# Conditioned two-stage block on one core: inner weight sums stored behind the second slot tile, and other places for the second group's transposes and outer sums

## The chip, the cores and the metric

The kernel runs on one core of a Trainium2 chip. A core has five engines with an instruction stream each: TensorE (PE; its weight loads, PEld, overlap matmuls), VectorE (DVE), ScalarE (ACT), GpSimd (POOL) and SyncE (SP), which here only issues transfers. ACT and POOL issue transfers too. Within an engine, instructions are taken in order; engines wait for each other, and for transfers, on semaphores. The metric is the device time of one execution in microseconds.

## What is computed

The input is 32 sequences of 128 tokens with 512 features, a condition vector for each sequence, and a mask. All is float32.

```python
m = mask[:, :, None]
shift, scale, gate_msa = jnp.split(silu(t) @ ada_w + ada_b, 3, axis=1)
norm = jnp.where(m, layernorm(x) * (1 + scale[:, None]) + shift[:, None], 0.0)
fwd = gelu(norm @ ssm_w1 + ssm_b1) @ ssm_w2 + ssm_b2
bwd = flip(gelu(flip(norm) @ bwd_w1 + bwd_b1) @ bwd_w2 + bwd_b2)
x = x + gate_msa[:, None] * jnp.where(m, fwd + bwd, 0.0)
shift_mlp, scale_mlp, gate_mlp = jnp.split(silu(t) @ ffada_w + ffada_b, 3, axis=1)
ff_norm = layernorm(x) * (1 + scale_mlp[:, None]) + shift_mlp[:, None]
h = gelu_tanh(ff_norm @ ff_w1 + ff_b1)
return x + gate_mlp[:, None] * (h @ ff_w2 + ff_b2)
```

The first half changes x only where the mask is set, and each token is treated alone. The second half is a feed-forward block (512 to 1024 to 512) over all 4096 tokens. The mask of this input is set at the padded tails of the sequences, a minority of the tokens.

## The kernel before, in words

**First half, on slots.** The masked tokens are numbered and packed into slots, 128 to a tile. Two tiles (0 and 1) are always done, two more (2 and 3) after them; later ones, if the mask asks for any, in a loop at the end. A slot tile is gathered from x, normalised and modulated (`modulated`), transposed (`transposed_slots`), put through the hidden layer (`hidden`: matmuls into a PSUM tile, GELU on ACT) and the projection (`project`, line 202: eight feature blocks of two matmuls each accumulate into one PSUM tile `po`). `finish_slots` and `keep_slots` then form the new token rows on DVE in three steps, bias (line 208), gate (line 210) and x (line 301), and store them in a DRAM tensor `x1_rows` (line 303): tiles 0 and 1 by the ACT queue, 2 and 3 by the SP queue.

**Second half, by pairs of groups.** The 32 sequences form eight groups of four; a pair p holds two groups. For each pair x is loaded (`load_side`, line 332) and the tokens that the first half changed are overwritten by indirect gathers from `x1_rows` on POOL (`take_first_half`, line 666). For pair 0 these can come only from the first 256 slots, so they wait for slot tiles 0 and 1 alone; those of pair 1 need tiles 2 and 3 too. Then come statistics (lines 698 to 704: variance on DVE, the power on POOL) and normalising (710). Group 0 is turned to feature rows by DVE blocks and transfers (`turned`, 737); group 1 of pair 0 by PE: `transposed` (line 726) writes four transposes for one block of features into a PSUM tile and DVE scales and shifts them into `xT[1]` (line 718).

**Fewer products.** Each of the two matrix products of a pair is done by a seven-product scheme on 2 x 2 blocks, and the first of them is done in two levels. The outer level forms sums of the token blocks (`TokenBlocks.one`, line 767: s1 = a21 + a22, s2 = s1 - a11, a21 = a11 - a21, s4 = a12 - s2) and of the weights. Two of the outer level's token blocks live in `s12`: P5 reads s1, P6 reads s2, and P1 and P2 read the plain `xT[0]`. The inner level, within each outer product, has sums of weight sums: `weight_sums(j)` for j = 1 to 4 makes seven blocks each on DVE (line 586) and stores them to DRAM (`t_rows`, lines 587 and 588: 512 KB and 384 KB), from which `load_weights` (line 844) brings them back. The buffers of sum 1 are two x tiles, reused by sum 4; sum 2 lies in the buffers of later fw2 sums, and sum 3 in the buffer `xn`, which group 0's normalised tokens take next.

`FirstProduct` runs seven streams (products of the inner level), each over the seven outer products (`phase`, line 898). The opening, written out by hand, is: product P1 of stream 1 and its seed (line 944), P1 of stream 2, then P2, P5 and P6 of stream 1, and so on. PSUM has three tile pools: `ps_t` (2 buffers, transposes), `ps_h` (3) and `ps_o` (3). A projection, and the accumulator `a` of a stream, come from `ps_o`; a new tile waits for the last reader of the buffer that it takes.

**What sets the order.** From the start of the first half to the end of the straight part everything stands under a manual schedule: each of the five engines runs its instructions in program order. A transfer takes one of eight completion semaphores in turn and waits until the transfer that had this semaphore before has landed, whichever queue issued it.

The opening of the second half, as the change finds it, is this:

```python
    finish_slots(2, h1, gs[0])
    po = project(1, h1, w2, "s3", {1: turn(0), 3: turn(1), 5: turn(2), 7: turn(3)})
    of_x[0] = TokenBlocks(0, xT)
    keep_slots(3, po, gs[1], lambda: of_x[0].one(1))
    for j in (2, 3):
        of_x[0].one(j)
```

`turn(k)` is the transpose of feature block k of group 1; the number in front is the feature block of the projection ahead of which it stands.

Of the kernel before, what the change touches and what calls it, by code (L numbers as in the profile page):

```python
# [22 lines left out]
def kernel(  # L23
# [49 lines left out]
    nc = tc.nc  # L73
# [70 lines left out]
    w2 = ssm.tile([P, HC, D], F32, name="w2")  # L144
# [18 lines left out]
    def group_of_tiles(name):  # L163
        return xnp.tile([P, G, D], F32, tag="xn", name=f"xn_{name}")
# [17 lines left out]
    def hidden(xT, n, w, bcol, func, name, pool, parts=range(HC)):  # L182

        h = []
        for f in parts:
            ph = ps_h.tile([P, 512], F32, tag="h", name=f"ph_{name}_{f}")
            for k in range(KC):
                nc.tensor.matmul(  # L188
                    ph[:, :n], w[:, k, ts(f, P)], xT[:, k, :], start=(k == 0), stop=(k == KC - 1)
                )  # L190
            t = pool.tile([P, n], F32, tag="h", name=f"h_{name}_{f}", bufs=HC + 2)
            nc.scalar.activation(t, ph[:, :n], func, bias=biasT[:, bcol + f : bcol + f + 1])  # L192
            h.append(t)
        return h

    def project(i, h, w, name, between=None):

        po = ps_o.tile([P, 512], F32, tag="o", name=f"po_{name}_{i}")
        for f in range(HC):
            if between and f in between:  # L200
                between[f]()
            nc.tensor.matmul(po, h[f][:, ts(i, P)], w[:, f, :], start=(f == 0), stop=(f == HC - 1))  # L202
        return po

    def gated(po, bias, gate, name, between=lambda: None):

        t = tp.tile([P, D], F32, tag="t", name=f"t_{name}")
        nc.vector.tensor_tensor(t, po, bias, ALU.add)
        between()
        nc.vector.tensor_tensor(t, t, gate, ALU.mult)  # L210
        return t

# [75 lines left out]
    def slot_part(at, j, pool, tag):  # L288
        return of_slots(pick, at, mod1, j, pool, tag, f"part{j}_s{at}")

    def keep_gate(at, gate):
        t = ssm.tile([P, D], F32, tag="gs", name=f"gs_{at}", bufs=2)
        nc.scalar.copy(t, gate)
        return t

    def finish_slots(at, h1, gate, between=None):
        keep_slots(at, project(at % (NC // 2), h1, w2, f"s{at}", between), gate)

    def keep_slots(at, po, gate, between=lambda: None):
        t = gated(po, b2, gate, f"s_{at}", between)  # L300
        nc.vector.tensor_tensor(t, t, xc[at], ALU.add)
        queue = nc.scalar if at < NC // 2 else nc.sync
        queue.dma_start(x1_rows[ts(at, P), :], t)
# [212 lines left out]
    b2 = ssm.tile([P, D], F32, name="b2")  # L516
# [43 lines left out]
    t_rows = dram.tile([4, P, 7, 2 * P], F32, name="t_rows")  # L560
    spare = [x_tile(f"{2 * G}_{n}") for n in range(2)]

    def in_blocks(t):
        return t.rearrange("p g (h f) -> p (g h) f", f=2 * P)

    t_sum = {
        1: [in_blocks(t) for t in spare],
        2: [t_2[:, 0], t_2[:, 2]],
    }
    t_sum[4] = t_sum[1]  # L570

    def sum_block(j, n):
        t = t_sum[j]
        return t[1][:, :3] if n == 2 else t[0][:, 2 * n : 2 * n + 2]

    def weight_sums(j):

        for n in range(3):
            b11, b12, b21, b22 = of_w.quarters(n, (0, 0), (0, 1), (1, 0), (1, 1))
            x, y = {  # L580
                1: lambda: (b12, b11),
                2: lambda: (b22, sum_block(1, n)),
                3: lambda: (b22, b12),
                4: lambda: (b21, sum_block(2, n)),
            }[j]()
            nc.vector.tensor_tensor(sum_block(j, n), x, y, ALU.subtract)
        nc.sync.dma_start(t_rows[j - 1, :, :4], t_sum[j][0])
        nc.sync.dma_start(t_rows[j - 1, :, 4:], t_sum[j][1][:, :3])


    h1 = []
    gs = []
    xn_s = []
    for c in range(2):
# [7 lines left out]
        if c == 1:  # L602
            transposed_slots(xn_s[0], xT_t[:, :, ts(0, P)], "s2")
    weight_sums(1)
    nc.vector.tensor_tensor(b2, b2, b2b, ALU.add)
    b2_row = dram.tile([1, D], F32, name="b2_row")
    nc.sync.dma_start(b2_row, b2[0:1, :])
    weight_sums(2)
    finish_slots(0, h1, gs[0])
    transposed_slots(xn_s[1], xT_t[:, :, ts(1, P)], "s3")  # L610
    t = in_blocks(group_of_tiles("tw_3"))
    t_sum[3] = [t[:, :4], t[:, 4:]]
    weight_sums(3)
    fw2_of = Weights(fw2, HC // 2, D // 2, t_2)
    fw2_of.combine(0, 1)
    nc.vector.tensor_scalar(modb_f[B : 2 * B], modb_f[B : 2 * B], 1.0, None, ALU.add)
    finish_slots(1, h1, gs[1])

    mod2 = const.tile([3 * B, D], F32, name="mod2")
    pm = ps_o.tile([P, 512], F32, tag="o", name="pm_f")  # L620
# [4 lines left out]
    gs = [keep_gate(c, slot_part(c, 2, ps_o, "o")) for c in (2, 3)]  # L625
# [29 lines left out]
    of_x = {}  # L655

    fb2_step = const.tile([P, D // 2], F32, name="fb2_step")
    nc.vector.tensor_tensor(fb2_step, fb2[:, D // 2 :], fb2[:, : D // 2], ALU.subtract)
    weight_sums(4)


    def take_first_half(p, xs, which=range(2 * G)):
# [59 lines left out]
    def transposed(g, xn, xT, k):  # L722

        ptr = ps_t.tile([P, 512], F32, tag="tr", name=f"ptr_{g}_{k}")
        for i in range(G):
            nc.tensor.transpose(ptr[:, ts(i, P)], xn[i][:, ts(k, P)], ident)
        for i in range(G):
            scale_and_shift(xT[:, k, ts(i, P)], ptr[:, ts(i, P)], k, g * G + i, True)
# [408 lines left out]
    for i in range(G):  # L1137
        t = stats[0].normalised(i, xn[:, :, i])
        nc.vector.transpose(t, t)
    h1 = hidden(xT_t, NH, w1, 0, AF.Gelu, "s1", ssm)  # L1140
# [13 lines left out]
    def turn(k):  # L1154
        return lambda: transposed(1, xn_b, xT[1], k)

    finish_slots(2, h1, gs[0])
    po = project(1, h1, w2, "s3", {1: turn(0), 3: turn(1), 5: turn(2), 7: turn(3)})
    of_x[0] = TokenBlocks(0, xT)
    keep_slots(3, po, gs[1], lambda: of_x[0].one(1))  # L1160
    for j in (2, 3):
        of_x[0].one(j)
    first_half.close()
    hp = straight.enter_context(tc.tile_pool(name="hp", bufs=1))
    gp = straight.enter_context(tc.tile_pool(name="gp", bufs=1))
# [165 lines left out]
    with tc.If(more > 0):  # L1331
        b2 = lp.tile([P, D], F32, name="b2_l")
# [10 lines left out]
        with tc.For_i(0, more, 1):  # L1343
# [12 lines left out]
            for half_no, (mod, was, wbs, bias, bcol, func) in enumerate(  # L1356
                (
                    (mod1, (ssm_w1, bwd_w1), (ssm_w2, bwd_w2), b2, col["ssm1"], AF.Gelu),
                    (mod2, (ff_w1,), (ff_w2,), fb2, col["ff1"], AF.Gelu_apprx_tanh),
                )  # L1360
            ):
                wa = lp.tile([P, KC, FF], F32, tag="wa", name=f"wa_l{half_no}")
                wb = lp.tile([P, HC, D], F32, tag="wb", name=f"wb_l{half_no}")
                for j, w in enumerate(was):
                    n = FF // len(was)
                    nc.sync.dma_start(wa[:, :, ts(j, n)], w.rearrange("(k p) f -> p k f", p=P))
                for j, w in enumerate(wbs):
                    n = HC // len(wbs)
                    nc.sync.dma_start(wb[:, ts(j, n), :], w.rearrange("(k p) f -> p k f", p=P))
                scale = of_slots(pick_l, 0, mod, 1, ps_o, "o", f"sc_l{half_no}")  # L1370
                shift = of_slots(pick_l, 0, mod, 0, ps_h, "h", f"sh_l{half_no}")
                xn_l = lp.tile([P, D], F32, tag="xnl", name=f"xn_l{half_no}")
                modulated(xl, scale, shift, f"l{half_no}", xn_l)
                xT_l = lp.tile([P, KC, P], F32, tag="xTl", name=f"xT_l{half_no}")
                transposed_slots(xn_l, xT_l, f"l{half_no}")
                h_l = hidden(xT_l, P, wa, bcol, func, f"l{half_no}", lp)
                gate_l = of_slots(pick_l, 0, mod, 2, ps_h, "h", f"gate_l{half_no}")
                t = gated(project(0, h_l, wb, f"l{half_no}"), bias, gate_l, f"l{half_no}")
                nc.vector.tensor_tensor(xl, xl, t, ALU.add)
# [58 lines left out]
```

## Time and profile before

| what | value |
|---|---|
| median of three runs | 469.02 us (468.23 to 469.58) |
| the profiled execution's own time | 469.54 us |
| its span, first to last instruction | 467.7 us |
| mean granted PE clock | 0.995 |
| busy: PE, PEld | 451.2 us (96%), 365.0 us (78%) |
| busy: DVE, ACT, POOL | 331.2 us (71%), 175.2 us (37%), 157.4 us (34%) |
| transfers | 70.41 MB, mean 151 GB/s |
| stores `t_rows<-x`, lines 587 and 588 | 2 each; median 6.9 and 11.2 us from issue to landing |
| stores `x_rows<-t_s` by ACT, by SP | 2 each; median 5.9 and 2.4 us |

The span is what the chain, the timeline and the stretches are measured on, in microseconds from its first instruction. In a timeline row the first number is the start, the second the duration, then engine, line, operation, output and inputs by the program's names (`t_s` the slot rows, `s` the sums of token blocks, `a_m` and `e_m` accumulators of the first product), shape, count, and in brackets how long the engine had been idle before, and what ended it. The chain of waits goes back from the last instruction to whatever released each step. A released wait is put down to the event that came last.

### The profile page before, as it was taken

The numbers are of one execution on the slowest core, as the hardware profiler recorded it, in microseconds if no ns is written. First come the engines' busy times: TensorE is split into PE (matmuls) and PEld (weight loads), VectorE is DVE, ScalarE is ACT, GpSimd is POOL, SyncE is SP. The second block draws the span as 40 slices with busy tenths as digits, with TensorE's granted clock in tenths as the row PEclk, the third lists the DMA queues.
The fourth block names the chain that finished last, engine by engine and source line by source line (L and its number), as shares of the span: only waits on it lengthen the run. The fifth ranks groups of instructions, "written<-read, shape, count | busy, mean of one in ns | idle before, by whom it ended". The sixth has DMA issues, their size and how long they took to land.

```text
span 467.7 us, 5829 instructions
## 1 busy us (share of the span) xinstructions
PE 451.2 (96%) x2000; PEld 365.0 (78%) x2000; DVE 331.2 (71%) x538; ACT 175.2 (37%) x380; POOL 157.4 (34%) x151
## 2 busy tenths in 40 slices
PE   5899999989999999999999999999999999999995
PEld 2385385468788888888888888888888888888884
DVE  4648757799668957997687498867874985434645
ACT  3121021635365173253643712535536134562000
POOL 6110054026975000289730003897100025660000
PEclk9999999899999999999999999999999999999999
DMA  8999943464504761934078438340973342212022
GB/s 278 385 408 360 400 173 51 73 221 158 162 5 161 120 103 64 309 139 163 1 201 107 99 104 302 93 152 3 228 100 78 126 168 72 87 67 114 0 79 104
DMA packets 82482, 70.41 MB, mean 151 GB/s; under 512 B 63168, under 2 KB 63696, under 8 KB 81426
## 3 DMA queue, kind: packets, MB, share of 16 engines
q1 hardware_dynamic: 67298, 57.42, 39.9%
q0 software_dynamic: 4256, 10.75, 6.8%
q10 hardware_dynamic: 10896, 1.84, 2.3%
q8 instruction: 17, 0.28, 0.2%
q14 instruction: 15, 0.12, 0.1%
HBM read 56.83 MB, written 13.17 MB: 150 GB/s over the span
## 4 chain that ended last, share of the span: by engine, by line
PE 63%; DMA 10%; POOL 9%; ACT 5%; issue 5%; DVE 5%; SPq 1%; POOLq 0%; DVEq 0%; ACTq 0%
PE a_o L1078 18%; PE e_o L1078 16%; PE a_m L898 14%; PE e_m L898 11%; DMA b2b<-in_L_cond_bwd_b_dram 4%; DMA t_rows<-x 2%; POOL x L666 2%; DMA x<-in_x_dram 2%; POOL hb L982 2%; ACT hb L860 2%; POOL rstd L704 2%; PE po_s L202 1%; POOL ha L949 1%; DMA x_rows<-t_s 1%; ACT ha L860 1%
## 5 line engine op out<-in xcount | busy, mean ns | idle before, releaser
L949 POOL TENSOR_TENSOR ha<-p_m,ha 128x512 f32<-128x512 f32 x20 | 27.2, 1362 | 152.5 <-ACT ha L956 143.3
L1078 PE MATMUL e_o<-fw,ha 128*128 128x256 f32 x256 | 57.9, 379 | 0.0
L720 ACT ACTIVATE xT<-xT,modT 128x128 f32<-128x128 f32 x112 | 44.0, 479 | 29.1 <-DMA xT<-xn 29.1
L1078 PE MATMUL a_o<-t,hb 128*128 128x256 f32 x240 | 54.1, 379 | 0.0
L1078 PEld LDWEIGHTS e_o<-fw,ha 128*128 128x128 f32 x256 | 48.6, 190 | 6.6
L1078 PEld LDWEIGHTS a_o<-t,hb 128*128 128x128 f32 x240 | 45.6, 190 | 6.2
L666 POOL DMA_INDIRECT x<-x_rows,slot_i x32 | 36.7, 1146 | 33.3 <-DMA x_rows<-t_s 22.9
L860 ACT ACTIVATE hb<-hb,biasT 128x256 f32<-128x256 f32 x64 | 29.0, 501 | 27.8 <-POOL hb L982 19.3
L912 ACT COPY p_m<-e_m 128x512 f32<-128x512 f32 x27 | 15.8, 586 | 52.2 <-PE e_m L898 52.2
L949 POOL TENSOR_TENSOR hb<-p_m,hb 128x512 f32<-128x512 f32 x20 | 27.8, 1391 | 21.0 <-DVE hb L928 20.6
L202 PE MATMUL po_s<-w,h_s 128*128 128x512 f32 x64 | 30.0, 616 | 0.0
L1078 PE MATMUL e_o<-fw,s 128*128 128x256 f32 x128 | 29.2, 381 | 0.5 <-DVE s L1032 0.2
L956 ACT COPY ha<-e_m 128x512 f32<-128x512 f32 x32 | 18.5, 578 | 28.4 <-PE e_m L898 26.7
L1078 PE MATMUL a_o<-fw,ha 128*128 128x256 f32 x128 | 28.9, 379 | 0.0
L1078 PE MATMUL a_o<-t,s 128*128 128x256 f32 x128 | 28.9, 379 | 0.0
L188 PE MATMUL ph_s<-xT_s,w 128*128 128x256 f32 x128 | 28.7, 382 | 0.0
L1078 PEld LDWEIGHTS e_o<-fw,s 128*128 128x128 f32 x128 | 24.1, 190 | 4.8 <-DVE s L1032 1.7
L188 PEld LDWEIGHTS ph_s<-xT_s,w 128*128 128x128 f32 x128 | 24.0, 190 | 4.7 <-ACT h_s L192 1.5
L923 DVE TENSOR_TENSOR e_m<-a_m,ha 128x512 f32<-128x512 f32 x20 | 13.9, 697 | 18.7 <-POOL ha L978 7.4
L1078 PEld LDWEIGHTS a_o<-t,s 128*128 128x128 f32 x128 | 24.3, 190 | 3.3
L1078 PEld LDWEIGHTS a_o<-fw,ha 128*128 128x128 f32 x128 | 24.3, 190 | 3.3
L860 ACT ACTIVATE ha<-e_m,biasT 128x256 f32<-128x256 f32 x48 | 20.1, 469 | 16.2 <-PE e_m L898 8.9
(205 smaller groups left out, 870.0 us busy)
## 6 DMA issues: line engine op xcount, KB each, us to landing
tw<-t_rows SPq DMA_DIRECT2D x16, 896.0 KB, 5.1
x<-in_x_dram SPq DMA_DIRECT2D x16, 512.0 KB, 7.0
gate<-gate_rows POOLq DMA_DIRECT2D x8, 1024.0 KB, 5.7
out_dram<-x SPq DMA_DIRECT2D x15, 512.0 KB, 3.4
xT<-xn SPq DMA_DIRECT2D x92, 64.0 KB, 2.8
fw<-in_L_cond_ff_w_dram SPq DMA_DIRECT2D x2, 2048.0 KB, 14.5
ada_f<-in_L_cond_ffada_w_dram SPq DMA_DIRECT2D x4, 768.0 KB, 15.6
ada_a<-in_L_cond_ada_w_dram SPq DMA_DIRECT2D x4, 512.0 KB, 4.6
```

The costliest lines, as they stand in the source:

```text
L188: nc.tensor.matmul(ph[:, :n], w[:, k, ts(f, P)], xT[:, k, :], start=(k == 0), stop=(k == KC - 1))
L202: nc.tensor.matmul(po, h[f][:, ts(i, P)], w[:, f, :], start=(f == 0), stop=(f == HC - 1))
L666: nc.gpsimd.indirect_dma_start(out=xs[i // G][i % G // 2][:, i % 2], out_offset=None, in_=x1_rows[:slots, :], in_offset=bass.IndirectOffse ...
L704: nc.gpsimd.tensor_tensor(self.rstd, ve, half[:, :G], ALU.pow)
L720: nc.scalar.activation(out, src, AF.Identity, bias=shift, scale=scale)
L860: nc.scalar.activation(dst[:, n], src[:, n], AF.Gelu_apprx_tanh, bias=biasT[:, f : f + 1])
L898: nc.tensor.matmul(bank[:, ts(n, QT)], self.w_block(j, product)[:, ts(n, P)], self.x_block(j, product), start=(product in ("P1", "P5") and ...
L912: nc.scalar.copy(p5, e)
L923: nc.vector.tensor_tensor(e, a, p5, add)
L949: nc.gpsimd.tensor_tensor(self.place(RESULT[j], c), self.p5[j], other, ALU.add)
L956: nc.scalar.copy(self.place(RESULT[j], c), src)
L1078: nc.tensor.matmul(part, src[:, k, ts(i, P)], w[product][:, k, :], start=(last and k == 0), stop=True, skip_group_check=True,)
```

## The change

It has three parts.

- `weight_sums(j)` no longer issues the two stores of its sums. A new function `store_weight_sums` does; it is called for sums 1, 3 and 2, in this order, behind `finish_slots(1)`, and for sum 4 directly behind `weight_sums(4)` as before. The sums themselves stay where they were on DVE.
- The four transposes of group 1 of pair 0 stand ahead of feature blocks 0, 2, 4 and 6 of slot tile 3's projection; before it was 1, 3, 5 and 7.
- On DVE, the outer sums 1 and 2 both stand ahead of the three steps of slot tile 3, and sum 3 behind them. Before, sum 1 stood between the first and the second step, and sums 2 and 3 behind the third. The argument `between` of `gated` and `keep_slots` falls away.

```diff
@@
-    def gated(po, bias, gate, name, between=lambda: None):
+    def gated(po, bias, gate, name):
 
         t = tp.tile([P, D], F32, tag="t", name=f"t_{name}")
         nc.vector.tensor_tensor(t, po, bias, ALU.add)
-        between()
         nc.vector.tensor_tensor(t, t, gate, ALU.mult)
         return t
@@
-    def keep_slots(at, po, gate, between=lambda: None):
-        t = gated(po, b2, gate, f"s_{at}", between)
+    def keep_slots(at, po, gate):
+        t = gated(po, b2, gate, f"s_{at}")
@@ weight_sums
             nc.vector.tensor_tensor(sum_block(j, n), x, y, ALU.subtract)
-        nc.sync.dma_start(t_rows[j - 1, :, :4], t_sum[j][0])
-        nc.sync.dma_start(t_rows[j - 1, :, 4:], t_sum[j][1][:, :3])
+
+    def store_weight_sums(*which):
+        for j in which:
+            nc.sync.dma_start(t_rows[j - 1, :, :4], t_sum[j][0])
+            nc.sync.dma_start(t_rows[j - 1, :, 4:], t_sum[j][1][:, :3])
@@
     finish_slots(1, h1, gs[1])
 
+    store_weight_sums(1, 3, 2)
+
     mod2 = const.tile([3 * B, D], F32, name="mod2")
@@
     weight_sums(4)
+    store_weight_sums(4)
@@
     finish_slots(2, h1, gs[0])
-    po = project(1, h1, w2, "s3", {1: turn(0), 3: turn(1), 5: turn(2), 7: turn(3)})
+    po = project(1, h1, w2, "s3", {0: turn(0), 2: turn(1), 4: turn(2), 6: turn(3)})
     of_x[0] = TokenBlocks(0, xT)
-    keep_slots(3, po, gs[1], lambda: of_x[0].one(1))
-    for j in (2, 3):
-        of_x[0].one(j)
+    of_x[0].one(1)
+    of_x[0].one(2)
+    keep_slots(3, po, gs[1])
+    of_x[0].one(3)
     first_half.close()
```

## The prediction

> **What bounds the kernel now.** Span 467.7 us, TensorE busy in 96% of it. I first read the page's forty slices: PE stands at 9 nearly everywhere but at both ends, so this edit can matter only where PE waits, or where it delays what PE will wait for. I then read the chain of waits over 20 to 128 us, where the edit lies:
>
> ```profile
> 44.66 11.10 DMA t_rows<-x
> ...
> 55.84 5.62 DMA x_rows<-t_s
> ...
> 71.08 1.05 POOL rstd L704
> ...
> 80.61 1.06 POOL rstd L704
> ...
> 96.64 0.33 SPq L303
> ...
> 100.02 9.63 DMA x<-in_x_dram
> ...
> 110.65 1.50 POOL x L666
> ...
> 121.75 1.06 POOL rstd L704
> ```
>
> Columns: start, duration, what. The second slot store (55.84) is released by the first inner-sum store; its landing at 61.46 releases the GpSimd gathers, two rounds of statistics and, at 82.39, the first transpose. Later the store of slot tile 3 (96.64) stands ahead of pair 1's x loads on SP's queue; those release gathers, and PE waits for that string at 127.26.
>
> The table by stretches says what the stores share (PE, PEld, DVE, ACT, POOL, clock, DMA share, GB/s):
>
> ```profile
> 60.00:61.00 1.00, 1.00 (x7) 0.87 (x6) 0.83 (x7) 0.00 (x0) 0.00 (x0) 1.00 0.74 281
> 61.00:62.00 1.00, 1.00 (x6) 0.90 (x5) 1.00 (x4) 0.47 (x1) 0.00 (x0) 1.00 0.17 68
> 84.20:87.60 3.40, 3.40 (x8) 1.63 (x7) 2.67 (x7) 1.61 (x3) 0.00 (x0) 0.50 0.80 157
> ```
>
> From 36 to 62 us the DMA share is 0.99 at 365 GB/s. The slot store lands as that backlog ends. The third line: after PE's pause (81.14 to 82.39, then spaced-out transposes) the granted clock is half for 3.4 us.
>
> The timeline around the outer sums shows who waits for whom:
>
> ```profile
> 93.47 0.68 DVE L208 TENSOR_TENSOR t_s<-po_s,b 128x512 f32<-128x512 f32 x1
> 94.07 1.22 DVE L767 TENSOR_TENSOR s<-xT 128x1024 f32<-128x1024 f32 x1
> 94.30 1.10 PE L898 MATMUL a_m<-xT,fw 128*128 128x256 f32 x4 [0.43 <-DVE t_s L208]
> 95.20 0.69 DVE L210 TENSOR_TENSOR t_s<-t_s,gs 128x512 f32<-128x512 f32 x1
> 95.92 0.69 DVE L301 TENSOR_TENSOR t_s<-t_s,xc 128x512 f32<-128x512 f32 x1
> 96.53 1.22 DVE L767 TENSOR_TENSOR s<-s,xT 128x1024 f32<-128x1024 f32 x1
> 97.80 1.13 PE L898 MATMUL a_m_alone<-s,t 128*128 128x256 f32 x4 [0.68 <-DVE s L767]
> ```
>
> The line at 94.30 decides: product 2's P1 goes into the accumulator buffer that held slot tile 3's projection, and waits for the bias add (L208) that reads it. Three o buffers rotate, and product 2's is the third tile taken after the projection's.
>
> **What the Trainium skill says.** "PSUM — Partial Sum Buffer", PSUM bank collisions raise a hardware error: two engines must not touch a bank at once, so a bank's reader is guarded by a semaphore. The wait at 94.30 agrees (0.43 us). "DMA: Bandwidth & Descriptors", Issuing engines are not separate DMA queues: SP's and ACT's transfers run on the same 16 engines and interleave. This agrees: the ACT-issued 256 KB slot stores take 5.6 and about 6 us inside the backlog, SP's uncrowded ones about 2. "TensorE: Matmul & The Clock Gate", Part 1: an idle window of some 3.4 us halves the clock; the row at 84.20 agrees with its length. In this trace a window with PE shown busy for 54% was followed by half clock, one with 70% was not.
>
> **The change part by part.**
>
> *Stores.* Six issues on SP (three of 512 KB, three of 384 KB) are written behind both slot stores, in the order sums 1, 3, 2; the little b2 row goes first. No arithmetic changes. SP does not wait for ACT's stores, so "behind" is program order, not time. What the order does decide is which earlier transfer a transfer must wait for: eight completion semaphores are reused, so each waits for the one eight before. Before: slot store 0 waited until 51.88 for an x load though its data were ready at 48.26; slot store 1 waited for the first store of sum 1, landed 55.76, though its data were ready at 55.57. After: store 0 leaves near 48.3, which frees nothing (the gathers need both); store 1 leaves near 55.6, a gain of 0.2. Its landing is then set by bytes: the DMA engines are full in both orders and the bytes ahead are the same, so it lands near 61.2. I take −0.1 us; ends: +0.3 (two sum stores issued just before it) to −2.2 (it gets in ahead of both sum-2 stores, 896 KB at about 400 GB/s). Sum 4 overwrites sum 1's buffers at 61.44; its stores landed by 57.1 before and should by about 60 now: covered by 1.4 us, and DVE then idles 2.5 us to 66.13, so nothing up to that.
>
> *Transposes.* They move from ahead of feature blocks 1, 3, 5, 7 to ahead of 0, 2, 4, 6. Before, block 0 ran to 81.14 and PE idled 1.25 us. Now projection 2 ends near 80.27 and PE idles about 2.1 us; block 0 (two matmuls, 0.87 us) follows the first transposes. Between successive transposes stand two blocks as before, so the four ends stay (last: 92.15). Behind the last now stand two blocks, not one: the projection ends at about 93.9, not 93.0. The four transposed scalings on DVE stay too; the next DVE slot is 93.47.
>
> *Outer sums.* DVE's work from 93.47 is the same six instructions: one 0.69 add, two 0.69 steps, three 1.22 sums (1.13 start to start). New order: sum 1 at 93.47, sum 2 at 94.6, bias add at 95.73 to 96.42, gate and slot row to 97.85, sum 3 to about 98.95 (before 98.88).
> Two things queue behind the later bias add:
> - PE's P1 of product 2: 94.30 becomes about 96.5, and P2, P5, P6 stand behind it in order at 0.86 each. P6 starts at 96.5 + 3 × 0.86 = 99.1, against 97.80: +1.3. Sum 2 is now ready at 95.7, but P6 can't use it.
> - SP's slot store 3: 96.64 becomes 97.85, +1.2; behind it two loads of weight sums and four x loads. So the x landing at 109.65, the gathers and the POOL string move by +1.2. The PE wait at 127.26 (1.03 us) is for that string, so this part isn't absorbed there.
> Both move together: +1.2, not their sum. If P1 had a free bank, the SP branch would still bring +1.2.
>
> *Clock.* Block 0 leaves the pause, so a window with 54% PE drops to about 44%: half clock, 3.4 us long and worth 3.4 / 2 = 1.7 us, stays or becomes more certain. The profiled execution already paid it. The three timed ones (468.23, 469.02, 469.58) differ by 1.35, which could be this; unshown. The new pause before P1 (94.8 to 96.5, 1.7 us) may bring a second such window; PE's 1.03 us of slack at 127 hides part.
>
> Sum against the profiled execution (469.54 us around a span of 467.7): −0.1 + 1.2 = +1.1, span 468.8, time 470.65. That execution lies 0.52 above the median of the runs shown; since I expect the half clock in nearly every execution after, I leave this in and say **470.7 us**, 0.36% above 469.02.
>
> **The rivals.**
> 1. *The second slot store gets ahead of the sum stores.* Store 0 going earlier pushes the last x load's landing from 54.5 to about 55.1 (256 KB at 400 GB/s), and the first sum-2 store waits for that landing: it leaves at about 55.15, the other at 55.5, the slot store at 55.6. A few tenths decide. If it passes both, its landing, the gathers and the transposes come up to 2.2 us earlier, PE has no pause at 81 and the half clock (1.7) goes: 469.54 + 1.2 − 2.2 − 1.7 = 466.8; if one, nearer 468. It beats the +1.2 from 1.2 us of earlier landing, or from 0.6 if that much spares the clock window. Against it: the backlog is full, and ACT's packets began 3.3 us after the issue in both slot stores. About 467.3 when it happens.
> 2. *The delay is absorbed.* PE waits for DVE several times between 98 and 103 and gathers have 0.3 us gaps; if these or the x loads give back 0.8 us, or half clock was not lost in either median, the time is about 469.2. Against: DVE and SP run in order and are late by the same amount.
> 3. *A second half-clock window behind the new pause.* 1.7 us at 97.9 to 101.3, of which about 1 can hide at 127 if POOL's operands are not late: about 472. For: the window would show PE busy about half. Against: the windows' phase may split the pause.
>
> **How the numbers follow.** The forecast case (470.0 to 471.4) gets 0.50, rival 1 0.20, rival 2 0.15, rival 3 0.15. A difference under 0.3% (1.4 us, so 467.6 to 470.4) is about what a measurement of this kernel can't tell from no change. Faster: rival 1, 0.20. Slower: rival 3 and about 0.36 of the forecast case, 0.51. Same: the other 0.14 and rival 2, 0.29. The range, 467.4 to 472.2, cuts the lower half of rival 1 and the top of rival 3; the forecast case's own is 470.0 to 471.4.
>
> **What would show it.** Right: slot store 1 issued near 55.6 and landing within 0.5 of 61.46; first transpose near 82.3; PE's P1 of product 2 waiting 1.5 to 2 us for the bias add; slot store 3 near 97.8; half clock again after 84. Wrong: the landing before 60.3 or no pause before the transposes (rival 1); P1 without its wait, in another buffer; x loads landing by 109.7 in spite of the later slot store 3 (rival 2); a second run of half clock near 98 (rival 3).

## The result, and the profile after

The changed kernel takes 473.95 us (median of 4 runs, 473.04 to 474.66) against 468.62 (4 runs, 467.52 to 469.58): 1.0113 times the time before, 95% interval 1.0084 to 1.0143. It is slower, by 5.3 us where the prediction had 1.7 and its range ended at 472.2. The profiled execution is the fastest of the four: 473.04 us, span 471.3, mean granted clock 0.993 (before: 469.54, 467.7 and 0.995).

The chain of waits of the changed kernel, the stretch that answers to the one shown of before:

```profile
55.51 5.89 DMA x_rows<-t_s
...
70.75 1.07 POOL rstd L709
...
94.05 0.61 DVE t_s L208
...
94.80 1.25 PE a_m L903 x4
...
115.11 2.95 DVE xT L842
...
119.06 1.68 PE e_m L903 x4
```

Its first part is the old one: the second slot store lands at 61.40 (before 61.46), statistics follow. Then it leaves the old road. Before, it went from the slot rows to SP, the x loads, the gathers and POOL. Now it stays on DVE and PE: the bias add (L208) releases P1 of stream 2, and an operation of DVE that nobody had in mind, 2.95 us long at 115.11, sits in front of PE's next long wait.

The timeline around the outer sums is close to what was forecast:

```profile
91.51 1.22 DVE L772 TENSOR_TENSOR s<-xT 128x1024 f32<-128x1024 f32 x1
92.82 1.23 DVE L772 TENSOR_TENSOR s<-s,xT 128x1024 f32<-128x1024 f32 x1
93.97 0.68 DVE L208 TENSOR_TENSOR t_s<-po_s,b 128x512 f32<-128x512 f32 x1
94.80 1.25 PE L903 MATMUL a_m<-xT,fw 128*128 128x256 f32 x4 [2.15 <-DVE t_s L208]
...
99.15 1.03 PE L903 MATMUL a_m_alone<-s,t 128*128 128x256 f32 x4
```

Both sums stand in front of the bias add, PE waits 2.15 us for it where it waited 0.43, and P6 starts at 99.15 against 97.80: 1.35 later (forecast 1.3). Up to P1 the starts are 1.7 to 2.0 us earlier than forecast, since this execution had no half clock at 84; P6 stands where it was forecast (99.1), because half clock behind the new pause takes the 1.7 us back. The stretches show it (columns as in the prediction: PE, PEld, DVE, ACT, POOL, clock, DMA share, GB/s):

```profile
60.00:61.00 1.00, 1.00 (x6) 0.90 (x5) 0.83 (x7) 0.00 (x0) 0.00 (x0) 1.00 0.78 302
61.00:62.00 1.00, 1.00 (x7) 0.87 (x6) 1.00 (x4) 0.47 (x1) 0.00 (x0) 1.00 0.27 110
84.20:87.60 3.40, 3.40 (x14) 1.77 (x13) 3.37 (x10) 1.82 (x4) 0.00 (x0) 1.00 0.64 136
95.55:98.95 3.40, 3.40 (x10) 2.69 (x9) 1.69 (x2) 0.58 (x1) 0.00 (x0) 0.51 0.50 154
119.45:122.85 3.40, 3.40 (x10) 2.66 (x9) 2.73 (x8) 0.59 (x1) 1.26 (x1) 0.51 0.00 0
```

The half clock that stood at 84.20 now stands at 95.6, behind the new pause of PE, and a second stretch of it follows at 119.5. Each is 3.41 us long and costs about half of that, 1.7 us, of PE's work.

What comes ahead of that second stretch is the larger half of the story. The timeline of the changed kernel, PE, DVE and POOL:

```profile
115.01 1.28 POOL L954 TENSOR_TENSOR ha<-p_m,ha 128x512 f32<-128x512 f32 x1
115.11 2.95 DVE L842 TENSOR_TENSOR xT<-xT,xn_sy 128x512 f32<-128x512 f32 x1
116.23 1.27 POOL L954 TENSOR_TENSOR hb<-p_m,hb 128x512 f32<-128x512 f32 x1
...
119.06 1.68 PE L903 MATMUL e_m<-xn_sy,tw 128*128 128x256 f32 x4 [2.41 <-DVE e_m L947]
```

and the same instructions before:

```profile
113.92 0.68 DVE L837 TENSOR_TENSOR xT<-xT,xn_sy 128x512 f32<-128x512 f32 x1
...
115.60 1.13 PE L898 MATMUL e_m<-xn_sy,tw 128*128 128x256 f32 x4
...
116.82 1.29 POOL L949 TENSOR_TENSOR ha<-p_m,ha 128x512 f32<-128x512 f32 x1
```

The DVE line is one of the inner level's token sums. Before, it took 0.68 us and ended 2.2 us ahead of POOL's two additions for stream 6 (`with_p5`, L949 before and L954 after). Now it begins 0.10 us behind the first of them and takes 2.95, to 0.56 us past the end of the second. The seed of the next accumulator (L947, at 118.32) is late by that, PE waits 2.41 us for it, and the half clock follows the wait.

PE's distance behind the kernel before, read at equal instructions of the two traces: 1.35 us at P6 of stream 1, 1.24 at the matmul that starts at 102.73 before and 103.97 after, 3.46 at the one of 115.60 and 119.06, and 5.14 at the one of 118.30 and 123.44. So a bit over 1 us comes from the pause, 2.2 from the long token sum, 1.7 from the half clock behind it. Before, PE waits 1.03 us at 127.26 for POOL's string; after, it doesn't, and that and some smaller waits come back. At the first matmul of the second product (138.00 before, 141.57 after) the distance is 3.6, and so is the difference of the spans. The other three timed runs show a clock of 0.988 or 0.989 instead of 0.993, which is one half-clock stretch more (3.41 / 2 of 471 is 0.36%), and are 0.9 to 1.6 us longer. That they had the one at 84 as well is likely and not shown, since they left no trace.

### The profile page after: what moved, and what is told of

Same layout as the page of the kernel before. It is cut to its first block, busy times and chain, and to the rows that moved or that the text cites. A ratio compares the mean times of both kernels' runs of the same rounds, so it can differ in the third digit from the quotient of the medians.

```text
span 471.3 us, 5827 instructions
## 1 busy us (share of the span) xinstructions
PE 452.8 (96%) x2000; PEld 366.9 (78%) x2000; DVE 333.4 (71%) x538; ACT 175.1 (37%) x380; POOL 156.8 (33%) x151
## 4 chain that ended last, share of the span: by engine, by line
PE 73%; DVE 8%; POOL 7%; ACT 5%; issue 4%; DMA 2%; POOLq 0%; DVEq 0%
PE a_o L1083 18%; PE a_m L903 16%; PE e_o L1083 16%; PE e_m L903 13%; PE po_s L202 4%; PE ph_s L188 3%; POOL hb L987 2%; ACT hb L865 2%; DMA x_rows<-t_s 1%; POOL rstd L709 1%; POOL x L671 1%; ACT ha L865 1%; POOL ha L987 1%; POOL ha L954 1%; DVE s L772 1%
## 5 line engine op out<-in xcount | busy, mean ns | idle before, releaser
L954 POOL TENSOR_TENSOR ha<-p_m,ha 128x512 f32<-128x512 f32 x20 | 27.2, 1361 | 152.5 <-ACT ha L961 143.3
L954 POOL TENSOR_TENSOR hb<-p_m,hb 128x512 f32<-128x512 f32 x20 | 27.8, 1388 | 22.5 <-DVE hb L933 22.2
L202 PE MATMUL po_s<-w,h_s 128*128 128x512 f32 x64 | 28.6, 592 | 0.0
```

Source lines behind the costliest of these rows:

```text
L954: nc.gpsimd.tensor_tensor(self.place(RESULT[j], c), self.p5[j], other, ALU.add)
```

## The experiments

The theory after the result: the new place of the outer sums does all the harm, a small part through the PE pause and the bigger part because DVE, now late, meets POOL. The rivals: the late slot store on SP (the prediction's second branch), the stores or transposes, or the pause and its half clock by themselves. Two of the kernels (e8, e12) add two matmuls whose result nobody reads; no kernel leaves a part of the computation out.

| kernel | runs | median us | ratio to before, 95% interval | token sum, us | POOL starts behind it by |
|---|---|---|---|---|---|
| before | 4 | 468.62 | | 0.68 | 2.90 |
| after | 4 | 473.95 | 1.0113 (1.0084 to 1.0143) | 2.95 | -0.10 |
| e1 stores alone | 20 | 466.81 | 0.9961 (0.9942 to 0.9979) | 0.68 | 1.57 |
| e2 transposes alone | 20 | 469.99 | 1.0011 (0.9993 to 1.0028) | 0.67 | 1.58 |
| e3 outer sums alone | 4 | 475.01 | 1.0134 (1.0094 to 1.0175) | 2.94 | -0.12 |
| e4 all but outer sums | 20 | 467.95 | 0.9979 (0.9959 to 0.9998) | 0.67 | 1.58 |
| e5 after, projection in another buffer | 12 | 468.37 | 0.9990 (0.9966 to 1.0014) | 0.68 | 4.54 |
| e6 after, POOL waits for the token sum | 20 | 469.83 | 1.0010 (0.9989 to 1.0031) | 0.68 | 1.23 |
| e7 after, bias add first | 12 | 468.87 | 0.9996 (0.9975 to 1.0017) | 0.67 | 4.54 |
| e8 after, pause filled | 12 | 469.96 | 1.0013 (0.9980 to 1.0047) | 0.67 | 2.89 |
| e9 e1, gathers put later on POOL | 12 | 470.80 | 1.0019 (0.9992 to 1.0046) | 1.39 | -0.43 |
| e10 e9, POOL waits as in e6 | 12 | 468.59 | 0.9993 (0.9975 to 1.0012) | 0.69 | 1.24 |
| e11 e1, buffer of e5 | 4 | 466.76 | 0.9938 (0.9915 to 0.9962) | 0.68 | 1.58 |
| e12 after, POOL waits and pause filled | 12 | 469.28 | 1.0007 (0.9988 to 1.0026) | 0.68 | 3.35 |

The last two columns are from each kernel's profiled execution: the duration of the token sum, and the start of POOL's first addition less the start of the token sum. The kernel before ran beside each batch, with medians of 469.23 (e1 to e4), 469.43 (e5 to e8) and 468.82 (e9 to e12), so kernels of different batches are compared by their ratios.

### The parts of the change alone: e1 to e4

e1 takes the new places of the stores and nothing else:

```diff
-        nc.sync.dma_start(t_rows[j - 1, :, :4], t_sum[j][0])
-        nc.sync.dma_start(t_rows[j - 1, :, 4:], t_sum[j][1][:, :3])
+    def store_weight_sums(*which): ...
     finish_slots(1, h1, gs[1])
+    store_weight_sums(1, 3, 2)
...
     weight_sums(4)
+    store_weight_sums(4)
```

> The kernel before with the stores alone moved (sums 1, 3, 2 behind slot tile 1). My theory (the outer sums' place on DVE does the harm): within 1 us of before; slot store 1 leaves 0.3 us earlier, lands within 0.5 us of the kernel before, no second half-clock window. Rival (the moved stores do the harm, by contention or by other transfers waited for): at least 2 us slower than before, with later gathers.

e2 takes the transposes:

```diff
-    po = project(1, h1, w2, "s3", {1: turn(0), 3: turn(1), 5: turn(2), 7: turn(3)})
+    po = project(1, h1, w2, "s3", {0: turn(0), 2: turn(1), 4: turn(2), 6: turn(3)})
```

> The kernel before with the transposes alone moved to blocks 0, 2, 4, 6. My theory: between 1 us faster and 0.7 us slower; block 0 fills the time between the first two transposes, so the half-clock window near 84 may be missing (worth 1.7 us), and the bias add, still first on DVE, waits about 0.4 us for the projection's last block. Rival (the transposes' place does the harm): 2 us slower or more.

e3 takes the outer sums:

```diff
-    keep_slots(3, po, gs[1], lambda: of_x[0].one(1))
-    for j in (2, 3):
-        of_x[0].one(j)
+    of_x[0].one(1)
+    of_x[0].one(2)
+    keep_slots(3, po, gs[1])
+    of_x[0].one(3)
```

> The kernel before with the outer sums alone moved (sums 1 and 2 ahead of slot tile 3's bias add). My theory: 3 to 6 us slower than before: P1 of stream 2 waits about 2 us for the bias add, a half-clock window follows that pause, and a token sum of DVE meets POOL's sums near 115 us and takes about 3 us instead of 0.7. Rival (stores or transposes do it, this costs only the 1.2 us that the prediction gave it): 0.8 to 1.6 us slower, no 3 us token sum.

e4 has the edits of e1 and e2 together, so it is the changed kernel with the outer sums back in their old order.

> The changed kernel with the outer sums put back as before (stores and transposes moved). My theory: within 1 us of the kernel before, 4 to 5 us faster than the changed kernel; no wait of P1 of stream 2 over 0.6 us. Rival (stores and transposes together do harm that neither does alone): at least 2 us slower than before.

The stores alone gain 0.39% (interval 0.21 to 0.58), the transposes alone show nothing that the runs can tell from no change, and the outer sums alone lose 1.34%. The changed kernel is 1.34% above e4 by the two ratios, so the harm is that of the outer sums, in both surroundings, and the stores hide a part of it. In e3's profile all is there again, some 2 us later: a PE wait of 3.00 us at the bias add, half clock from 97.1, and a token sum of 2.94 us beside POOL's additions.

The gain of the stores came by another way than the prediction's. The second slot store left at 55.29 instead of 55.84 and took 5.76 us instead of 5.62; the first transpose began at 81.98 instead of 82.39. That is 0.4 us. The rest of what can be named is the clock: mean 0.9985 over e1's runs against 0.9968 in the runs beside it, which is 0.17% or 0.8 us, and e1's profiled execution has no half clock between its ends. Between the two profiled executions (469.54 and 467.16, 2.4 apart) 0.4 are the earlier transposes and 1.7 the half clock; PE's wait of 1.03 for POOL's string at 127.26 is gone as well, but a wait of 1.07 for a load of weight sums (`tw<-t_rows`, at 202.87), which the kernel before doesn't have there, takes that back. Over all runs a third to a half of the gain (1.8 us by the ratio, 2.4 by the medians) has no place that is shown; the wait at 127.26 is a candidate.

### Is it the pause or the slot store: e5 and e7

e5 is the changed kernel with slot tile 3's projection in `ps_h`, so that P1 of stream 2 has an accumulator of its own while the bias add and slot store 3 stay as late:

```diff
-    def project(i, h, w, name, between=None):
+    def project(i, h, w, name, between=None, pool=None):
-        po = ps_o.tile([P, 512], F32, tag="o", name=f"po_{name}_{i}")
+        po = (pool or ps_o).tile([P, 512], F32, tag="h" if pool else "o", ...)
...
-    po = project(1, h1, w2, "s3", {0: turn(0), ...})
+    po = project(1, h1, w2, "s3", {0: turn(0), ...}, ps_h)
```

> The changed kernel with slot tile 3's projection in a buffer of the other accumulator pool (ps_h), so that P1 of stream 2 no longer waits for the bias add; DVE's order is that of the changed kernel. My theory (the buffer wait makes PE late and throws the later work against POOL): P1 follows without a pause, P6 about 1.5 us sooner, no half clock behind it, no 3 us token sum: 466.5 to 470, that is 4 to 7 us faster than the changed kernel. Rival (the late slot store 3 is the cause): within 1.5 us of the changed kernel.

The timeline of e5:

```profile
94.08 1.03 PE L903 MATMUL a_m<-xT,fw 128*128 128x256 f32 x4
...
95.56 0.68 DVE L208 TENSOR_TENSOR t_s<-po_s,b 128x512 f32<-128x512 f32 x1
```

P1 runs ahead of the bias add, without a wait. Slot store 3 leaves at 97.7, as late as the prediction had it, and the median is that of the kernel before. In e7 the bias add comes first and the two outer sums behind it, ahead of the other steps of the slot tile:

```diff
-    of_x[0].one(1)
-    of_x[0].one(2)
-    keep_slots(3, po, gs[1])
+    keep_slots(3, po, gs[1], lambda: (of_x[0].one(1), of_x[0].one(2)))
```

> The changed kernel with the bias add first, then outer sums 1 and 2, then gate, x and sum 3: the buffer is released as early as before, slot store 3 stays late. My theory: P1 waits under 0.6 us, no collision, within 1.5 us of the kernel before (467.5 to 470). Rival (late slot store 3 and its x loads carry the 1.2 us that the prediction gave them): at least 1 us slower than the kernel before, with gathers 1 us later against PE's P6.

Slot store 3 leaves at 98.5, later still, P1 has no pause, and the median is again that of before. So the late slot store is not what costs 5 us: POOL's additions come late (118.10 in e5, 118.85 in e7), and that takes them further from the token sum, 4.54 us in both.

It doesn't follow that the branch through SP is free. The profiled executions of e5 and e7 (470.61 and 471.47) are the slowest of their twelve, and in them POOL's late string does hold up PE. In e5:

```profile
119.41 0.70 DVE L928 TENSOR_TENSOR e_m<-a_m,ha 128x512 f32<-128x512 f32 x1 [1.21 <-POOL ha L954]
...
120.17 1.13 PE L903 MATMUL e_m<-xn_sy,tw 128*128 128x256 f32 x4 [0.34 <-DVE e_m L928]
```

A second such wait, of 1.35 us, follows at 128.54. The chain of waits goes back from there over POOL's additions, the gathers and the x loads to slot store 3 at 97.72, and e7 has the same two waits (0.34 and 1.36 us). e4, which has the stores and transposes but not the outer sums, has no wait of PE between 105 and 149. Against e4, whose stores gain as theirs do, e5 is 0.11% and e7 0.17% slower by the ratios, 0.5 and 0.8 us, with intervals that overlap. A price near the prediction's 1.2 us is therefore neither shown nor excluded.

### Is it the meeting with POOL: e6

e6 is the changed kernel with one small copy on POOL, of one element, in front of the two additions of stream 6 in the first pair. It reads the block that the token sums finish, so POOL comes behind them:

```diff
+    mark = const.tile([1, 1], F32, name="mark")
...
+                    if j == 6 and self.p == 0:
+                        _, a12, a11 = self.x.parts(3, self.sx[6], (1, 0), (0, 0))
+                        nc.gpsimd.tensor_copy(mark, a11[0:1, 0, 0:1])
                     self.with_p5(j, "12")
```

> The changed kernel with POOL's sums of stream 6 of pair 0 made to wait for DVE's last token sum (one 1-element copy on POOL that reads it), so that the two engines no longer work at once there. Theory A[...]: the token sum takes 0.7 us again, the 2.4 us wait of PE behind it goes, and the time is 1.5 to 3.5 us below the changed kernel, though POOL starts its sums up to 1 us later. Theory B (the 3 us token sum is a symptom that costs nothing, the pause ahead of P1 is all): within 0.7 us of the changed kernel.

Its timeline:

```profile
117.69 0.68 DVE L843 TENSOR_TENSOR xT<-xT,xn_sy 128x512 f32<-128x512 f32 x1
...
118.77 0.18 POOL L922 COPY mark<-s 1x1 f32<-1x1 f32 x1 [1.23 <-ACT hb L866]
118.92 1.26 POOL L958 TENSOR_TENSOR ha<-p_m,ha 128x512 f32<-128x512 f32 x1
```

The token sum is 0.68 us again, though the pause before P1 (2.15 us in this profile too) and its half clock are still there. The ratio falls from 1.0113 to 1.0010. About 1.0% or nearly 5 us of the changed kernel's time is the meeting with what it brings, more than the 1.5 to 3.5 us that were expected, and what stays against e4 is 0.3% or 1.5 us (the intervals overlap), which would be the pause with its half clock. The profiled execution of e6 (471.78) is one of its slow ones, with two half-clock stretches in a row from 81.6 and one at 98.7. PE reaches the first matmul of the second product 59.58 us behind its first transpose in the changed kernel, 58.27 in e6 and 54.24 in e4, with two, three and one half-clock stretches on the way. An estimate that takes off 1.7 us for each leaves 56.2, 53.2 and 52.5: some 3 us for the meeting without its half clock, and 0.6 for the rest.

### Filling the pause: e8 and e12

e8 is the changed kernel with two matmuls of 512 columns whose result nobody reads, in front of P1 of stream 2:

```diff
     now.seed(1)
+    spare_ps = ps_t.tile([P, 512], F32, tag="tr", name="spare_ps")
+    for n in range(2):
+        nc.tensor.matmul(spare_ps, ident, fw1[:, 0, :512], start=True, stop=True)
     now.do(2, "P1")
```

> The changed kernel with two matmuls of 512 columns, whose result nobody reads, put into PE's pause ahead of stream 2's P1 (about 1.7 us of work into a 2.15 us pause). Theory (the pause costs a half-clock window besides itself): no half clock between 95 and 100 us, granted clock up by 0.003 to 0.004, time 0.8 to 1.7 us below the changed kernel. Rival (half clock there hides under DVE's work): within 0.5 us of the changed kernel, with the collision at 115 still there in both cases.

In its profile the added matmuls run for 1.88 us at 93.95, P1 follows at 96.26 with 0.43 us of its wait left, no half clock comes behind it, and the token sum is 2.89 us ahead of POOL. P1 still waits for the bias add, and the meeting doesn't come about, which the expectation had not foreseen: the median is 4 us below the changed kernel's, not 0.8 to 1.7. Set beside e3, whose profile has half clock at 84 as e8's has: P1 starts 0.9 us earlier in e8 (96.26 against 97.14), the token sum 2.6 us earlier (114.89 against 117.50), POOL's addition 0.4 later (117.78 against 117.38). The 1.7 us between 0.9 and 2.6 are what a half-clock stretch is worth, so in these two profiles it is the half clock behind the pause that completes DVE's delay. The times of e8 spread over 6.8 us (466.68 to 473.46), though, and the profiled one (472.39) lies near the upper end without either effect. In it PE waits 1.03 us at 128.22 for a DVE step that POOL's string releases, and 0.76 and 0.95 us at 206.92 and 299.31 for loads of weight sums. e12 has the fill and e6's copy on POOL:

> The changed kernel with both: POOL's sums of stream 6 wait for DVE's last token sum, and two unread matmuls fill PE's pause ahead of stream 2's P1. What is left of the change's harm is the pause itself, without half clock behind it and without the collision: by the prediction's 1.2 us, 0.5 to 1.5 us above the changed kernel without the moved sums (467.95), so 468.4 to 469.5, and 0.3 to 1.4 us under the kernel with the POOL wait alone. If half clock behind the pause costs nothing, as slow as that one (469.8).

1.0007 against e6's 1.0010: with the meeting gone, filling the pause gains nothing that can be told. What is left against e4 is 0.28% or 1.3 us, with intervals that just overlap. That isn't the late P1 alone: in e12's profile PE also waits 1.39 us at 129.60 for a step that POOL's string releases.

### The meeting without the pause: e9 and e10

e9 starts from e1, which has neither the pause nor the late sums, and puts two of POOL's gathers behind the two additions, so that these run earlier:

```diff
-            put(2, 6, take_first_half, p + 1, x_next, range(G, G + 2))
+            put(*((3, 0) if p == 0 else (2, 6)), take_first_half, p + 1, x_next, range(G, G + 2))
```

> The stores-only kernel with two of pair 1's gathers (for tiles 4 and 5 of x) put behind POOL's sums of stream 6 of pair 0, so that these sums start some 2 us sooner and meet DVE's token sums; nothing waits longer for a buffer and no engine gets more work. Theory A (the meeting of DVE and POOL is enough to cost microseconds): a token sum takes 2 to 3 us instead of 0.7, and the time is 1.5 to 4.5 us above the stores-only kernel (468.3 to 471.5). Theory B (PE's pause ahead of stream 2's P1 is needed too): within 0.8 us of the stores-only kernel.

Its timeline:

```profile
113.71 1.27 POOL L955 TENSOR_TENSOR ha<-p_m,ha 128x512 f32<-128x512 f32 x1 [1.01 <-ACT p_m L918]
114.14 1.39 DVE L843 TENSOR_TENSOR xT<-xT,xn_sy 128x512 f32<-128x512 f32 x1
114.94 1.71 POOL L955 TENSOR_TENSOR hb<-p_m,hb 128x512 f32<-128x512 f32 x1
115.45 1.48 DVE L843 TENSOR_TENSOR s<-s,xn_sy 128x256 f32<-128x256 f32 x1
...
117.60 1.82 PE L904 MATMUL e_m<-xn_sy,tw 128*128 128x256 f32 x4 [1.91 <-DVE e_m L948]
```

The same two engines meet, with POOL's first addition 0.43 us ahead, and both lose. The two DVE operations (0.68 and 0.42 us elsewhere) take 1.39 and 1.48, POOL's second 1.71 instead of 1.28, PE waits 1.91 us and half clock follows from 117.9. The time is 470.80 against e1's 466.81, 0.58% more by the ratios; in its own batch e11, which differs from e1 by a buffer, is 0.81% below it. Its runs fall in two groups: six with a mean clock of 0.991 to 0.993 take 471.40 to 472.51 us, six with 0.995 to 1.000 take 467.31 to 470.19; whether the engines meet in the second group too isn't known. e10 adds e6's copy to it:

> The same with POOL's sums of stream 6 made to wait for DVE's last token sum (one 1-element copy on POOL). Theory A: the token sum is back at 0.7 us and the time within 1 us of the stores-only kernel (466 to 468). If the later gathers were what costs, it is as slow as the kernel without this wait.

The token sum is back at 0.69 and no half clock is in its profile. Its ratio is 0.26% under e9's, with intervals that overlap, and 0.32% above e1's: it goes the expected way, and did not come back to the stores-only time. Its profile shows a price of the later gathers: PE waits 1.34 us at 126.00 for a DVE step that POOL's later additions release, a wait that neither e1's profile nor e9's has.

### The best version: e11

e11 is e1 with the buffer of e5, the two edits that helped or did no harm.

> The stores-only kernel with slot tile 3's projection in a buffer of ps_h: the 0.43 us wait ahead of stream 2's P1 goes. Up to 0.4 us faster than the stores-only kernel if that wait is on the path; the same if P6 is still held by outer sum 2 (P6 waited 0.68 us for it before), which I hold for likelier: 466 to 467.5.

466.76 us, 0.9938 (0.9915 to 0.9962): faster than both kernels. Against e1 (0.9961 with 20 runs) no difference is shown; the stores alone are what pays.

## Why the prediction was wrong in size

The sign was right, for only a part of the reasons. The step that failed is the term for the outer sums: it priced the waits, at +1.2 us, and put at nothing what DVE's later work would run beside. There the runs show a token sum of 2.95 us instead of 0.68, a PE wait of 2.41 us behind it and a half-clock stretch worth 1.7 us behind that. By the prediction's own steps:

**Stores (-0.1).** Mis-sized. In the changed kernel the second slot store left at 55.51 and landed at 61.40, both within what was named as right, and the transposes began 0.4 us earlier. (The first left at 50.14, not near 48.3; as forecast, nothing came of that.) But alone the stores gain 0.39%, 1.8 us. The prediction had the key for part of that: its rival 1 said that a little earlier landing may spare the half-clock stretch. The forecast took that stretch for a cost of nearly every execution, and e1 shows that it is lost in some executions and not in others.

**Transposes (0).** Right: the ends of the four keep their spacing, PE's pause ahead of them is 1.81 us (forecast 2.1), and e2 is at 1.0011 (0.9993 to 1.0028).

**Outer sums, P1 (+1.2 to +1.3).** Right in mechanism: a wait of 2.15 us for the bias add. That P6 came 1.35 us later is luck in part: P1 itself started only 0.50 us later than before, since the half clock at 84 was gone, and the half clock behind the pause added the rest. e5, which only gives P1 another accumulator, brings the median back to that of the kernel before.

**Outer sums, SP.** Open in size: "If P1 had a free bank, the SP branch would still bring +1.2." In e5 slot store 3 is late by the forecast amount, PE waits 0.34 and 1.35 us for POOL's string in the profiled execution, and over all runs the kernel is at 0.9990, 0.5 us above e4 with overlapping intervals. In the changed kernel the branch had no part, and PE's 1.03 us wait at 127.26 was gone. "Both move together" failed: between before and after, DVE's token sum moved by +1.19 us (113.92 to 115.11) and POOL's first addition by -1.81 (116.82 to 115.01). Slot store 3 left at 96.13 instead of 96.64, earlier than before, because the half clock at 84 was gone (the rest of the 1.81 came in the x loads and gathers behind it), and the half clock behind the pause then held back PE and DVE and not POOL.

**Clock.** The stretch at 84 "stays or becomes more certain": not in the profiled execution. Rival 3, a second window near 98 behind the new pause, was the better forecast of the mechanism (half clock from 95.6); its price of 472 missed what the late DVE then runs into.

**The missing step.** The prediction's sum moved DVE's work by over a microsecond and asked only who waits for it, not what it would then run beside. The Trainium skill states the answer, in "SBUF — State Buffer", Who interferes with whom: a VectorE instruction with both inputs in SBUF contends with a GpSimd instruction that reads SBUF, and the one that is not first blocks. The runs agree: 2.95 and 2.94 us instead of 0.68 where the token sum starts behind POOL's addition, 0.68 where POOL is made to come 1.2 us later (e6), and the meeting made on purpose in e9. It needed one look at the timeline at 112 to 119: a token sum of DVE, two additions of POOL on its far side, 2.9 us apart and fed by different strings. That the lock on a shared port is the cause is what the skill says; the runs show the meeting and its price. It was on view in the trace before, too:

```profile
102.30 1.27 POOL L949 TENSOR_TENSOR hb<-p_m,hb 128x512 f32<-128x512 f32 x1 [20.64 <-DVE hb L928]
102.58 3.21 DVE L827 TENSOR_TENSOR sx<-xT 128x512 f32<-128x512 f32 x2
103.53 1.71 POOL L949 TENSOR_TENSOR ha<-p_m,ha 128x512 f32<-128x512 f32 x1
```

Two block sums of DVE (0.68 us each in the clear) take 3.21 us beside POOL's first two additions. They release nothing that PE waits for, so this price was hidden in every kernel here.

**What stays open.** Which of the changed kernel's timed runs had which half-clock stretches; a third to a half of the stores' gain; what the branch through SP costs once P1 doesn't wait; and how the 1.3 to 1.5 us that e12 and e6 keep against e4 divide between the pause and POOL's string.

## What to carry to other kernels

When a step moves an engine's work, look not only at who waits for it but at what the other engine of the pair VectorE and GpSimd does at its new time: the start of one less the start of the other, read from the timeline, is a margin, and here losing one of 2.9 us cost about 5 us. A delay of one engine isn't a delay of all: a pause and the half clock behind it hold up TensorE and those who feed it, while transfers and GpSimd keep going, and such margins close by the sum. Where a wait is for a buffer, try another buffer before another order.

## What the runs showed of the hardware

- A VectorE addition with two inputs in SBUF, 128x512 float32, took 2.95 and 2.94 us when it started 0.10 and 0.12 us behind the first of two successive GpSimd additions of 1.28 and 1.27 us, 0.68 otherwise. When it started 0.43 us behind (e9), the two engines took turns: 1.39 us on VectorE, 1.71 on GpSimd. An addition on VectorE with one input in PSUM kept its length beside GpSimd (line 923 of the kernel before, 0.70 us at 118.48, beside the addition that runs from 118.05 to 119.33), and so did the statistics, with one input (line 698, 0.69 at 119.09).
- "TensorE: Matmul & The Clock Gate", Part 1, has a free-running activity window of 3.4 us. The runs agree with the length: in the profiled executions every half-clock stretch inside the kernel lasts 3.41 us or twice that, and stretches of one execution are whole multiples of 3.41 us apart (95.61 and 119.51: seven). On the grid of 3.41 us that the stretches give, the window ahead of a half-clock stretch had PE busy, as the profile shows it, between 12% and 54%. Windows of 42, 48, 60 and 68% weren't followed by one, so this share doesn't decide alone. Pauses of 1.3 us (with spaced-out transposes behind it) to 3.0 us stood in the windows ahead of half clock.
- Two executions of one kernel can therefore differ by whole half-clock stretches of 1.7 us. That isn't the only source: the 20 runs of e1 lie between 464.97 and 469.87, and both ends show a mean clock of 1.000. Six of the fourteen profiles (those of e1, e2 and e8 to e11) have waits of PE of 0.68 to 1.41 us for a load of weight sums, the others none; whether these waits make the spread isn't shown.
